# An attention and feed-forward kernel: the stack copies on two queues, the reading of folded maxima held until the division ahead is done, tensor steps taken first in a turn, and the first projections in another order

## The chip, the cores and the metric

The kernel runs on one core of one Trainium2 chip. The metric is device time in microseconds (us) of one execution, of which the median over several runs is taken. The engines are named as in the profile: PE (matrix multiply; PEld is its weight load), DVE (VectorE), ACT (ScalarE), POOL (GpSimd) and SP (SyncE, which here only issues DMAs). A trailing q, as in SPq, marks an engine's own instruction queue.

## The reference

The block is a normalised attention and a normalised gated feed-forward, each added to its input. B is 4, S is 1024, D is 256, 16 heads of 16, hidden width 1024; all in float32. The feed-forward weights hold only -1, 0 and 1, with a scale for each output row.

```python
def attn(x, Wqkv, Wout):                      # x: (4, 1024, 256)
    q, k, v = split_heads(x @ Wqkv.T)         # 16 heads of 16
    scores = einsum('bhqd,bhkd->bhqk', q, k) / sqrt(16)
    p = exp(clip(scores - max(scores), -50, 50))
    out = einsum('bhqk,bhkd->bhqd', p / (sum(p) + 1e-6), v)
    return merge_heads(out) @ Wout.T

def ffn(x):
    h = silu(x @ w1.T * s1) * (x @ w2.T * s2)
    h = gelu(h @ h1.T * t1)
    h = gelu(h @ h2.T * t2)
    return h @ w3.T * s3

x = x + layernorm(attn(layernorm(x), Wqkv, Wout))
x = x + layernorm(ffn(layernorm(x)))
```

## The kernel before

**Attention.** It fills roughly the first half of the span. Work goes by batch `b`, group `g` of four heads, and half `h` of 512 queries; such a triple is a *unit*, and there are 32. A unit has 16 tiles: eight chunks `c` of 128 keys, twice two heads. For one tile PE makes the scores of two heads in PSUM (`s`, L534), and ACT takes the exponential of 128x1024 values (`e`, L535) into a ring of eight. PE then weighs the values (`acc`, L542) with `vaug`, which holds the group's values with a column of ones, so that the sum of the exponentials comes out beside the output.

**Stacks.** Queries and keys are kept as a high and a low part (`cq`, with the low part made by DVE in L394), so that one matmul of 64 rows makes the four products of parts. For that the parts of a group's heads must lie below one another in the tiles `sq` and `sk` (`stacks`). They get there by DMA: `copies` gives 16 copies for the keys and 16 for the queries of a group (L482), 64 KB each; `stack(b, g)` turns these 32 into steps. There are two sets of stacks, used by turns (`g % 2`), so the copies of a group start when the group two before it is done (`unit_end`). For `g` of 2 or 3, the first copy has to follow the projection of the second half of the channels (`later["qk1"]`).

**Maxima and division.** The reference adds 1e-6 to the sum of exp(score - max), while the kernel's exponentials are taken without the maximum, so the small term has to be scaled by the largest exponential. DVE keeps a running maximum over the first 128 queries of each half (`top`, L554). `divide` then writes `top` to DRAM by SP (L572), reads it back turned into `folded` (step `back`, L575), folds it on DVE (L579, L580) and divides (step `run`: `em` in L584, `den`, then `on` in L565). `folded` has one buffer; `o` and `top` have two.

**Order of the work.** Instructions stand in each engine's queue in the order in which the program emits them. A loop emits in *turns*: in each, the scores and exponentials of three tiles, some of the weighing, and then `side.take`, which fits in side work: the next batch's layer norm, transposes (`pt`), projections (`p`, `pv`), flags (`pn`), the output projection (`py`), the divisions, the stack copies, and the rounding of the feed-forward weights on POOL. Side work stands in chains of `Step`s. A step has a gap in turns to the one before, may be a tensor step (at most one of these a turn, all through one PSUM bank, `misc`), may have an amount of DVE work that counts against the turn's room, and may have a condition `ready`. `take` goes through the chains in order, divisions first (`self.first`), and runs what is due.

**Queues.** SP issues the stack copies, the loads of `x` and of the output weights `wo` (L222), and both DMAs of a division. POOL computes `rstd` of each layer norm (L107), copies values to `vaug` (`slots`, L512), and loads, rounds and stores the feed-forward weights (`round_weights`, L270 to L275, and `round_corners`, L291 to L312).

**The head.** Before the loop, the first batch's layer norm, transposes and the projections of the first group are written out by hand. `queues` there deals the copies to ACT, POOL and SP: of each eight, one, four and three. The Q part of the weights is packed by `compact(0)` on ACT, emitted ahead of the first Q projection. The first `v[0]` is emitted before the loop; `v[1]` and the first `slots` are side work.

The feed-forward part, from some 590 us on, runs from a list of its own and is not touched.

Of the kernel before, what the change touches and what calls it, by code (L numbers as in the profile page):

```python
# [21 lines left out]
DH = 16  # L22
# [15 lines left out]
NQ = 512  # L38
# [91 lines left out]
def tile_fast(ctx: ExitStack, tc: tile.TileContext, x, wqk, wv, wo, w1, w1s, w2, w2s, h1, h1s, h2, h2s, w3, w3s, out, bad):  # L130
# [65 lines left out]
    with ExitStack() as actx, ExitStack() as rctx:  # L196
# [11 lines left out]
        def compact(w):  # L208
            nc.scalar.copy(wqk_sb[:, :, w], padded[:, :, w, :, 0:DH])  # L209
# [8 lines left out]
        def load_rest():  # L218


            def load(out, in_):
                return lambda: nc.sync.dma_start(out=out, in_=in_)  # L222

            def load_half(b, h):
                return lambda: load_x(b, [h])

            rest = [load_half(2, h) for h in range(NH)]
            for c in range(DC):
                for h in range(HPT):
                    r = SLOT * (HPT * c + HPG * (h % GPT) + h // GPT)  # L230
                    rest.append(load(wo_sb[DH * h : DH * (h + 1), c, :], wo[r : r + DH, :]))
            rest += [load_half(b, h) for b in range(3, B) for h in range(NH)]
            rest += [load(scales[name], w) for name, w in (("w1", w1s), ("w2", w2s), ("h1", h1s), ("h2", h2s))]
            return rest + [load(w3s_sb, w3s.partition_broadcast(P))]
# [253 lines left out]
        def few(run_all, n):  # L488


            def some(part):
                return lambda: [run() for run in part]

            return [Step(some(run_all[i : i + n]), 1, False) for i in range(0, len(run_all), n)]

        def stack(b, g):

            outstanding.append((b, g))

            def done():  # L500
                stacked[g % 2] = b, g
                outstanding.remove((b, g))

            steps = few([lambda copy=copy: copy(nc.sync) for w in (1, 0) for copy in copies(g, w)], 4 if g < GPT or later["qk1"] == b else 6)
            steps[0].ready = lambda: g < GPT or later["qk1"] == b
            return steps + [Step(done, 0, False)]

        def slots(b, g, t0=0, t1=NT):


            def run():
                nc.gpsimd.tensor_copy(  # L512
                    vaug[g % 2][:, t0:t1, :, 0:DH], cv[:, t0:t1, HPG * DH * g : HPG * DH * (g + 1)].rearrange("p t (h e) -> p t h e", e=DH)
                )
                slotted[g % 2] = b, g, t1

            return run
# [38 lines left out]
        def quotients(g, h, em, o):  # L556

            o = o.rearrange("p (j s) -> p j s", s=SLOT)
            den = small.tile([P, NQ // SLOT], F32, tag="den", name="den")
            n = P // SLOT  # L560
            nc.vector.scalar_tensor_tensor(den[:, 0:n], em, SM_EPS, o[:, 0:n, DH], ALU.mult, ALU.add)
            nc.vector.tensor_copy(den[:, n:], o[:, n:, DH])
            nc.vector.reciprocal(den, den)
            e = DH * (g % GPT)
            nc.vector.tensor_mul(on[h][:, g // GPT, :, e : e + DH], o[:, :, 0:DH], den.unsqueeze(2).to_broadcast([P, NQ // SLOT, DH]))  # L565

        def divide(g, h, o, top):


            there = shuffle.tile([HPG, P, P], F32, tag="top", name="top_d")  # L570
            folded = work.tile([P, P // SLOT, P], F32, tag="folded", name="folded", bufs=1)
            nc.sync.dma_start(out=there.rearrange("i k q -> k i q"), in_=top.rearrange("p u n q -> p (u n) q"))  # L572

            def back():
                nc.sync.dma_start(out=folded, in_=there.rearrange("i (k s) q -> (i k) s q", s=P // SLOT))  # L575

            def fold():
                for n in (2, 1):
                    nc.vector.tensor_max(folded[:, 0:n], folded[:, 0:n], folded[:, n : 2 * n])  # L579
                nc.vector.transpose(folded[:, 1], folded[:, 0])  # L580

            def run():
                em = small.tile([P, P // SLOT], F32, tag="em", name="em")
                nc.vector.tensor_reduce(em, folded[:, 1].rearrange("p (j k) -> p j k", k=SLOT), AX.X, ALU.max)  # L584
                quotients(g, h, em, o)

            return [Step(back, 2, False), Step(fold, 2, False, work=1.2), Step(run, 1, False, work=1.4)]

        def divide_last(g, h, o, top):

# [88 lines left out]
        class Side:  # L679
# [34 lines left out]
            def take(self, room=math.inf, spare=0.0):  # L714

                self.slot += 1
                free, heavy = True, False
                step = self.next_tensor(self.slot)

                self.room = min(self.room, 0.5) + room - (step.work if step and not step.heavy else 0)  # L720
                for chain in self.first + self.rest:
                    while (step := self.due(chain, self.slot, free)) and (step.tensor or not step.work or self.room > spare):
                        chain[0].pop(0)
                        chain[1] = self.slot
                        if step.split:
# [600 lines left out]
        normalise = [steps[: TPQ // 2] for steps in xt]  # L1326
        for step in norm[0] + normalise[0] + norm[1]:
            step.run()
        for h in range(NH):
            for step in xt[h][TPQ // 2 :]:  # L1330
                step.run()
            for w, step in zip((1, 0), qk[0][h]):
                if (h, w) == (0, 0):
                    compact(0)
                step.run(0, 1)
                for i, copy in enumerate(copies(0, w, h * NQ, (h + 1) * NQ)):
                    copy(queues[i % len(queues)])
                if w and h + 1 < NH:
                    for step in normalise[h + 1]:
                        step.run()  # L1340
        stacked[0] = 0, 0
        v[0].run()
        alone = False
        load_x(1)
        early = [v[1], Step(slots(0, 0, 0, NT // 2), 0, False)]
        side.add(early + v[2:] + [Step(slots(0, 0), 0, False), Step(slots(0, 1), 0, False)] + sum(qk[1], []) + [Step(lambda: later.update(qk1=0, v=0), 0, False), Step(lambda: add_flags(flags[0] + flags[1]), 0, False)])
# [293 lines left out]
```

## Time and profile before

| what | us |
|---|---|
| median of 3 runs | 1218.02 |
| the runs | 1216.05 to 1218.22 |
| the profiled execution | 1217.59 |
| its span, first to last instruction | 1215.7 |
| PE, ACT, DVE, POOL busy | 1162.8, 885.8, 841.0, 207.8 |
| first exponential starts | 27.35 |

The busy times tell how much of the span an engine has work; a busy PE is also one whose matmuls run slowly. In an answer on waits, each line gives the waiting engine and line, what it waited for, and us in total, how often, and the longest. In a timeline a line gives start and duration in us, engine, line, instruction, what it writes and reads, its shapes and count, and in brackets the idle time of the engine before it and what ended it. A line of a table by stretches gives the busy time of each engine with the number of its instructions, then the granted clock of PE as a share of full speed, the DMA engines' busy share and GB/s.

### The profile page before, as it was taken

To read this page: it belongs to the slowest core of one execution; us is meant where nothing else is said; L and a number is where in the kernel's file an instruction comes from. 1 tells how busy PE (TensorE), PEld (TensorE's weight loads), DVE (VectorE), ACT (ScalarE), POOL (GpSimd) and SP (SyncE) were. 2 spreads that over 40 slices of the span, in tenths; PEclk is the share of its full clock that TensorE was granted. 3 is DMA by queue.
4 is the path that set the end of the run, shared out by engine and by line. 5 is a ranking of instruction groups with operands and counts; after the bars stand their busy time and mean duration, and the time that the engine had idled before them with its cause. 6 is when DMAs were issued, how large, how long until landed. Compare 5 with 4: busy or idle time off the path is not lost.

```text
span 1215.7 us, 21265 instructions
## 1 busy us (share of the span) xinstructions
PE 1162.8 (96%) x7994; PEld 708.4 (58%) x7994; DVE 841.0 (69%) x1500; ACT 885.8 (73%) x1049; POOL 207.8 (17%) x279
## 2 busy tenths in 40 slices
PE   7899999999999999999999999999999999999995
PEld 2333333333333333333478889888898887988885
DVE  3485668777687756867775757767669576695756
ACT  3798899878989989999456565675756757556661
POOL 6221135435354432100010000000000000000000
PEclk9999999999999999999999999999999999999998
DMA  4776755756666765454304442254523536135411
GB/s 136 179 184 159 166 149 133 189 133 171 158 152 165 187 170 141 92 138 148 105 1 140 138 139 77 97 169 144 188 72 99 176 124 201 60 104 173 142 50 38
DMA packets 78672, 163.66 MB, mean 135 GB/s; under 512 B 14688, under 2 KB 40928, under 8 KB 78560
## 3 DMA queue, kind: packets, MB, share of 16 engines
q1 hardware_dynamic: 68624, 131.27, 39.3%
q0 software_dynamic: 9408, 30.42, 7.9%
q8 instruction: 65, 1.06, 0.4%
q10 hardware_dynamic: 528, 0.52, 0.2%
q14 instruction: 47, 0.39, 0.1%
HBM read 98.71 MB, written 29.88 MB: 106 GB/s over the span
## 4 chain that ended last, share of the span: by engine, by line
PE 69%; ACT 10%; DVE 9%; DMA 4%; SPq 3%; issue 3%; ACTq 0%; POOL 0%; POOLq 0%; DVEq 0%
PE ph L1034 34%; PE acc L542 10%; PE pg L955 8%; ACT e L535 8%; PE s L534 6%; PE pz L1142 4%; PE p L321 3%; SPq L482 2%; DVE top L554 2%; PE py L321 2%; DMA x<-in_x_dram 1%; PE pv L321 1%; DMA sq<-cq1lo 1%; DVE st L97 1%; PE fpt L898 1%
## 5 line engine op out<-in xcount | busy, mean ns | idle before, releaser
L535 ACT ACTIVATE e<-s 128x1024 f32<-128x1024 f32 x512 | 483.0, 1044 | 52.5 <-PE s L534 42.8
L542 PE MATMUL acc<-e,vaug 128*32 128x512 f32 (+1 forms) x2424 | 259.0, 540 | 3.2 <-POOL vaug L512 3.2
L534 PE MATMUL s<-sq,sk 64*128 64x512 f32 x1024 | 189.2, 446 | 24.0 <-ACT e L535 17.8
L534 PEld LDWEIGHTS s<-sq,sk 64*128 64x128 f32 x1024 | 87.4, 185 | 170.7 <-ACT e L535 141.8
L1034 PE MATMUL ph<-hi,sq 128*128 128x512 f32 x448 | 177.7, 397 | 0.0
L1034 PE MATMUL ph<-lo,sq 128*128 128x512 f32 x448 | 176.7, 394 | 0.0
L1034 PE MATMUL ph<-hi,sk 128*128 128x512 f32 x448 | 176.6, 394 | 0.0
L1034 PE MATMUL ph<-lo,sk 128*128 128x512 f32 x448 | 176.4, 394 | 0.0
L107 POOL TENSOR_TENSOR rstd<-ve,minus_half 128x4 f32<-128x4 f32 (+1 forms) x34 | 38.2, 1123 | 729.8 <-DVE ve L105 625.4
L554 DVE TENSOR_TENSOR top<-top,e 128x512 f32<-128x512 f32 x192 | 138.9, 723 | 24.5 <-ACT e L535 18.7
L542 PEld LDWEIGHTS acc<-e,vaug 128*32 128x32 f32 x2424 | 62.0, 110 | 121.0 <-issue 108.2
L929 DVE TENSOR_TENSOR lo<-g,hi 128x1024 fp32r<-128x1024 f32 x48 | 58.8, 1225 | 58.1 <-ACT hi L925 58.0
L1034 PEld LDWEIGHTS ph<-lo,sk 128*128 128x128 f32 x448 | 84.1, 188 | 20.0
L1034 PEld LDWEIGHTS ph<-hi,sk 128*128 128x128 f32 x448 | 84.1, 188 | 20.0
L1034 PEld LDWEIGHTS ph<-hi,sq 128*128 128x128 f32 x448 | 84.1, 188 | 19.5
L1034 PEld LDWEIGHTS ph<-lo,sq 128*128 128x128 f32 x448 | 84.2, 188 | 19.3
L1022 ACT ACTIVATE c<-ph,h_scale 128x512 f32<-128x512 f32 x64 | 40.6, 685 | 55.7 <-PE ph L1034 55.7
L929 DVE TENSOR_TENSOR lo<-c,hi 128x1024 fp32r<-128x1024 f32 x48 | 58.2, 1219 | 25.8 <-ACT hi L925 25.8
L957 ACT ACTIVATE sg<-pg,w_scale 128x512 f32<-128x512 f32 x64 | 43.9, 688 | 42.0 <-PE pg L955 38.4
L321 PE MATMUL p<-xT,wqk_sb 128*32 128x512 f32 x512 | 67.4, 606 | 4.5 <-ACT wqk_sb L209 2.6
L958 DVE SCALAR_TENSOR_TENSOR g<-pg,w_scale,sg 128x512 f32<-128x512 f32 x64 | 47.7, 747 | 22.1 <-ACT sg L957 22.1
L1142 PE MATMUL pz<-w_sb,hi 128*128 128x256 f32 x256 | 60.0, 279 | 0.0
(183 smaller groups left out, 1729.0 us busy)
## 6 DMA issues: line engine op xcount, KB each, us to landing
sq<-h_f SPq DMA_DIRECT2D x56, 512.0 KB, 3.7
sk<-h_f SPq DMA_DIRECT2D x56, 512.0 KB, 4.4
w<-in_h_dram POOLq DMA_DIRECT2D x32, 256.0 KB, 5.2
h_f<-wr POOLq DMA_DIRECT2D x16, 512.0 KB, 4.3
x<-in_h_dram SPq DMA_DIRECT2D x16, 512.0 KB, 3.5
top_d<-top SPq DMA_DIRECT2D x30, 256.0 KB, 2.4
folded<-top_d SPq DMA_DIRECT2D x30, 256.0 KB, 3.2
h_f<-wr POOLq DMA_DIRECT2D x16, 384.0 KB, 3.8
```

The lines of the kernel that those rows point to most:

```text
L321: nc.tensor.matmul(o[j : j + SLOT, :], w[:, j : j + SLOT], i, **flags)
L534: nc.tensor.matmul(s[:, a, :], stacks[1, g % 2, u][r, c * P : (c + 1) * P], stacks[0, g % 2, u][r, h * NQ : (h + 1) * NQ], start=True, sto ...
L535: nc.scalar.activation(pair(k)[:, u], s, AF.Exp)
L542: nc.tensor.matmul(acc[SLOT * i : SLOT * (i + 1), q0:q1], vaug[g % 2][:, c, i, :], pair(k)[:, i // 2, i % 2, q0:q1], start=c == 0 and q0 = ...
L554: nc.vector.tensor_max(top, top if c > 1 else pair(k - 2)[:, :, :, 0:P], pair(k)[:, :, :, 0:P])
L929: nc.vector.tensor_sub(self.lo[i].t, self.raw[i].t, self.hi[i].t.bitcast(F32))
L955: nc.tensor.matmul(p[:, k, :], homes[n][d][:, m * P : (m + 1) * P], half[:, d, :], start=d == j == 0, stop=d == DC - 1 and j == 1)
L957: nc.scalar.activation(sg, p[:, 0, :], AF.Silu, scale=scales["w1"][:, m : m + 1])
L958: nc.vector.scalar_tensor_tensor(x[i, h][c // 2].t[:, c % 2, :], p[:, 1, :], scales["w2"][:, m : m + 1], sg, ALU.mult, ALU.mult)
L1022: nc.scalar.activation(o.t[:, j, :], (o.t if src is None else src)[:, j, :], AF.Gelu, scale=scale[:, m : m + 1])
L1034: nc.tensor.matmul(p[:, j, :], w, half, start=start and c == n == 0, stop=c == HC // 2 - 1 and n == 1, skip_group_check=True,)
L1142: nc.tensor.matmul(p[:, j, :D], half[:, (t0 + j) * P : (t0 + j + 1) * P], homes["w3"][c], start=c == order[0] and n == 0, stop=c == order[ ...
```

## The change

- `stack`: the 32 copies go to SP, POOL, SP and so on by turns, six in a step; before, all went to SP, and a step had four or six.
- `load_rest`: the 16 loads of `wo` are issued by POOL, not SP.
- `divide`: the step that reads the maxima back waits, by a condition, until the division of the unit ahead has been emitted.
- `take`: chains whose next step is a tensor step are gone through first, then all chains as before.
- The head: `compact(0)` is emitted before the first K projection, the normalisation of the second half is split around that projection, ACT's copies of the first Q are emitted after the second half's transposes, `v[1]` is emitted before the loop, and the first group's `slots` run on DVE in two halves (the copy for the second group stays on POOL).

```diff
-            def load(out, in_):
-                return lambda: nc.sync.dma_start(out=out, in_=in_)
+            def load(out, in_, queue=nc.sync):
+                return lambda: queue.dma_start(out=out, in_=in_)
...
-                    rest.append(load(wo_sb[DH * h : DH * (h + 1), c, :], wo[r : r + DH, :]))
+                    rest.append(load(wo_sb[DH * h : DH * (h + 1), c, :], wo[r : r + DH, :], nc.gpsimd))
...
-            steps = few([lambda copy=copy: copy(nc.sync) for w in (1, 0) for copy in copies(g, w)], 4 if g < GPT or later["qk1"] == b else 6)
+            turns = (nc.sync, nc.gpsimd, nc.sync)
+            runs = [copy for w in (1, 0) for copy in copies(g, w)]
+            steps = few([lambda copy=copy, queue=turns[i % len(turns)]: copy(queue) for i, copy in enumerate(runs)], 2 * len(turns))
...
-        def slots(b, g, t0=0, t1=NT):
+        def slots(b, g, t0=0, t1=NT, engine=nc.gpsimd):
...
-                nc.gpsimd.tensor_copy(
+                engine.tensor_copy(
...
+        divided = {"made": 0, "done": 0}
+
         def divide(g, h, o, top):
...
+            mine = divided["made"]
+            divided["made"] += 1
...
                 quotients(g, h, em, o)
-
-            return [Step(back, 2, False), Step(fold, 2, False, work=1.2), Step(run, 1, False, work=1.4)]
+                divided["done"] += 1
+
+            begun = Step(back, 2, False)
+            begun.ready = lambda: divided["done"] == mine
+            return [begun, Step(fold, 2, False, work=1.2), Step(run, 1, False, work=1.4)]
...
-                for chain in self.first + self.rest:
+                chains = self.first + self.rest
+                for chain in [c for c in chains if c[0] and c[0][0].tensor] + chains:
...
-        for h in range(NH):
+
+        def project_first(h, w):
+
+            qk[0][h][1 - w].run(0, 1)
+            runs = [(queues[i % len(queues)], copy) for i, copy in enumerate(copies(0, w, h * NQ, (h + 1) * NQ))]
+            for queue, copy in runs:
+                if queue is not nc.scalar:
+                    copy(queue)
+            return [copy for queue, copy in runs if queue is nc.scalar]
+
+        def turn_first(h):
+
             for step in xt[h][TPQ // 2 :]:
                 step.run()
-            for w, step in zip((1, 0), qk[0][h]):
-                if (h, w) == (0, 0):
-                    compact(0)
-                step.run(0, 1)
-                for i, copy in enumerate(copies(0, w, h * NQ, (h + 1) * NQ)):
-                    copy(queues[i % len(queues)])
-                if w and h + 1 < NH:
-                    for step in normalise[h + 1]:
-                        step.run()
+
+        turn_first(0)
+        compact(0)
+        normalise[1][0].run()
+        for copy in project_first(0, 1):
+            copy(nc.scalar)
+        normalise[1][1].run()
+        held = project_first(0, 0)
+        turn_first(1)
+        for copy in held:
+            copy(nc.scalar)
+        for w in (1, 0):
+            for copy in project_first(1, w):
+                copy(nc.scalar)
         stacked[0] = 0, 0
-        v[0].run()
+        for step in v[0:2]:
+            step.run()
+        slots(0, 0, 0, NT // 2, nc.vector)()
         alone = False
         load_x(1)
-        early = [v[1], Step(slots(0, 0, 0, NT // 2), 0, False)]
-        side.add(early + v[2:] + [Step(slots(0, 0), 0, False), Step(slots(0, 1), 0, False)] + sum(qk[1], []) + ...
+        side.add(v[2:] + [Step(slots(0, 0, NT // 2, NT, nc.vector), 0, False), Step(slots(0, 1), 0, False)] + sum(qk[1], []) + ...
```

More of the change, by code (lines that the diff above doesn't have):

```diff
@@ L1328, in tile_fast @@
             step.run()
-        for h in range(NH):
+        def project_first(h, w):
[6 more added lines that the diff above has]
+        def turn_first(h):
             for step in xt[h][TPQ // 2 :]:
                 step.run()
-            for w, step in zip((1, 0), qk[0][h]):
-                if (h, w) == (0, 0):
-                    compact(0)
-                step.run(0, 1)
-                for i, copy in enumerate(copies(0, w, h * NQ, (h + 1) * NQ)):
-                    copy(queues[i % len(queues)])
-                if w and h + 1 < NH:
-                    for step in normalise[h + 1]:
-                        step.run()
+        turn_first(0)
[11 more added lines that the diff above has]
+                copy(nc.scalar)
         stacked[0] = 0, 0
-        v[0].run()
+        for step in v[0:2]:
+            step.run()
+        slots(0, 0, 0, NT // 2, nc.vector)()
         alone = False
         load_x(1)
-        early = [v[1], Step(slots(0, 0, 0, NT // 2), 0, False)]
-        side.add(early + v[2:] + [Step(slots(0, 0), 0, False), Step(slots(0, 1), 0, False)] + sum(qk[1], []) + [Step(lambda: later.update(qk1=0, v=0), 0, False), Step(lambda: add_flags(flags[0] + flags[1]), 0, False)])
+        side.add(v[2:] + [Step(slots(0, 0, NT // 2, NT, nc.vector), 0, False), Step(slots(0, 1), 0, False)] + sum(qk[1], []) + [Step(lambda: later.update(qk1=0, v=0), 0, False), Step(lambda: add_flags(flags[0] + flags[1]), 0, False)])
         begin(0)
```

## The prediction

> **What bounds the kernel now.** I read the page's busy times first, then the waits of TensorE, then the timeline at each long wait.
>
> ```profile
> PE 1162.8 (96%) x7994; PEld 708.4 (58%) x7994; DVE 841.0 (69%) x1500; ACT 885.8 (73%) x1049; POOL 207.8 (17%) x279
> ...
> L535 ACT ACTIVATE e<-s 128x1024 f32<-128x1024 f32 x512 | 483.0, 1044 | 52.5 <-PE s L534 42.8
> ```
>
> PE is busy 96% of the span. The attention stage runs from the first exponential at 27.35 us to the last, which ends near 591 us; after it, the windows show PE busy at 50.00 of 50 us almost throughout, so the feed-forward stage cannot give or take much. In attention, 512 exponentials have 483 us of ACT; ACT waits for PE more than for anything else. PE runs one program in a fixed order, so **the stage is the sum of PE's work and PE's idle time**. What the change can win is idle PE time, and matmuls that ran at a lower clock. The waits of PE name it:
>
> ```profile
> PE s L534 <- DMA sq<-cq1lo: 5.3, 3, 2.8
> PE acc L542 <- POOL vaug L512: 3.2, 2, 1.6
> PE p L321 <- ACT wqk_sb L209: 2.6, 1, 2.6
> PE py L321 <- DVE norm L426: 2.1, 2, 1.8
> ```
>
> Columns: total us, times, longest. (The larger PE wait, 17.8 us in 52 pieces of some 0.4 us for ACT's exponentials, is the normal hand-over and stays.) The timeline puts the four in place. The head, with the idle time before each in brackets:
>
> ```profile
> 14.94 3.43 PE L321 MATMUL p<-xT,wqk_sb 128*32 128x512 f32 x16 [2.63 <-ACT wqk_sb L209]
> 18.30 1.23 PE L363 MATMUL pt<-ident,xn 128*128 128x128 f32 x8
> ...
> 32.38 1.06 PE L542 MATMUL acc<-e,vaug 128*32 128x512 f32 x8 [1.61 <-POOL vaug L512]
> ```
>
> The first Q projection waits for `compact(0)`, which sits on ACT behind two DMA issues, and takes 3.43 us; the K projection before it, of the same 16 matmuls, took 1.92. Then two late stacks:
>
> ```profile
> 83.95 3.14 SPq L482 DMA_DIRECT2D sq<-cq1hi  x4
> 87.14 0.57 SPq L222 DMA_DIRECT2D wo_sb<-in_wo_dram  x1
> ...
> 99.87 1.07 PE L534 MATMUL s<-sq,sk 64*128 64x512 f32 x2 [1.88 <-DMA sq<-cq1lo]
> ...
> 229.19 3.39 SPq L482 DMA_DIRECT2D sq<-cq1lo  x4
> 240.04 0.33 SPq L575 DMA_DIRECT2D folded<-top_d  x1
> 240.42 2.41 SPq L482 DMA_DIRECT2D sq<-cq1hi  x4
> 242.88 2.50 SPq L482 DMA_DIRECT2D sq<-cq1lo  x4
> ...
> 246.70 0.47 PE L534 MATMUL s<-sq,sk 64*128 64x512 f32 x1 [2.77 <-DMA sq<-cq1lo]
> ```
>
> These are two causes. From 69.69 to 98.56 SP issues without a pause (32 stack copies, seven loads of `wo`, three DMAs of divisions): SP itself is full. From 232.6 to 240.04 SP stands still in front of L575, which overwrites `folded` while the unit before has not read it (L584 ran at 239.74); eight copies wait behind it. Both times the clock drops:
>
> ```profile
> 98.00:104.00 6.00, 4.12 (x20) 1.36 (x22) 4.57 (x14) 3.05 (x4) 0.00 (x0) 0.72 0.27 55
> 244.00:251.00 7.00, 4.13 (x21) 1.30 (x21) 3.68 (x10) 2.96 (x3) 0.00 (x0) 0.76 0.53 100
> ```
>
> The column after POOL is the granted clock: 0.28 x 6 and 0.24 x 7 us are 1.7 us lost each, on top of the idle time.
>
> **What the Trainium skill says.** "TensorE: Matmul & The Clock Gate", What's actually happening: a lightly used window of 3.4 us lets the clock fall to half. The trace agrees: three falls in the stretch up to 251 us, each next to a PE wait of 1.88 to 2.77 us, each worth 1.7 us. "DMA: Bandwidth & Descriptors", SWDGE vs HWDGE vs iDMA: a DMA on POOL has its descriptors written by the GpSimd cores. "SBUF — State Buffer", Who interferes with whom: POOL is shut out while certain VectorE operations run. The trace of before shows only mildly longer POOL issues: 0.487 us for the head's copies, 0.54 to 0.81 for the weight DMAs later.
>
> **The change, part by part.**
>
> *Head.* `compact(0)` moves ahead of the first K projection's copies: ACT ends the second `xT` at 10.82, compacts by 11.5, so Q's matmuls follow K's at 12.3 and, with PE busy, at full clock: done by 14.3. The second half's `xn` is split around the K residual: its `rstd` is there at 12.74, then half of 1.42 us, L394's 0.69, the other half: 14.9. So the transposes start at 14.9, not 18.30: **3.4 us**. From there the old distances hold, since the held ACT issues (1.2 us) now follow `xT`. The Q copies must be there when PE, after v[0] and v[1], reaches the scores near 25 us: POOL has 8 + 8 copies of 0.49 us from 13.3, so 21.1, plus 2.2 to land, 23.3; SP's 6 + 6 of 0.6 land near 23.7. Just in time. v[1] is only moved. The values go to `vaug` on DVE, idle there, not on POOL behind 16 copies: the 1.61 us vanish, and about 0.8 of the later 1.56 us (POOL began 0.13 us after `cv`, copied twice for 1.95). With 0.3 for a wait on `cv`: head **6.1 us**.
>
> *Stack copies.* 15 stacks of 32 copies. Before: 4 a turn in 8 turns, all on SP at 0.59 to 0.69 us. After: 21 on SP, 11 on POOL, 6 turns. SP's share per turn stays at 4, but ends two turns (some 6.5 us) earlier; 16 `wo` loads leave it too. The stall at 98 (1.88 + 1.7) and one of 0.62 at 136.7 go: **4.2 us**. POOL takes 165 copies and 16 loads: 181 x 0.49 to 0.81 = 89 to 147 us, on an engine with under 12 of each 20 us busy: hidden, if its order allows (rivals).
>
> *`begun.ready`.* L575 is not issued before the other division was; SP no longer stands in front of it and nothing is added to SP. The late stack at 244: 2.77 + 1.7 = **4.5 us** (the earlier copies would cover part of this too; I count it once). The wait it adds is in the order of emission: the unit's division comes later, and with it `o` and `top`, both with two buffers; 0, while a unit is about 17 us and one division 5 turns.
>
> *Tensor steps first.* PE gets the same number of steps; what alters is DVE's order in a turn: PSUM is emptied ahead of the division and statistics.
>
> ```profile
> 343.75 1.93 PE L321 MATMUL py<-wo_sb,oT 128*32 128x256 f32 x32 [1.84 <-DVE norm L426]
> ```
>
> Here L426 waited behind em, den, `on` and two statistics (340.43 to 343.0) with the one misc bank held: **1.8 us** gone. The order was not seen elsewhere; bound it by -2 to +4 us (another such stall with its clock).
>
> Sum: 6.1 + 4.2 + 4.5 + 1.8 = 16.6 us. A new order of 500 turns makes some new wait: I charge one of the kind at 98, 3.6 us. Net **13 us**. The profiled execution took 1217.59 us (span 1215.7), 0.4 below the median 1218.02. 1217.6 - 13 = **1204.6**.
>
> **Rivals.**
>
> *POOL delivers late (slower).* POOL runs in order, and waits:
>
> ```profile
> 169.36 0.72 POOL L309 TENSOR_TENSOR wr<-w 128x256 fp32r<-128x256 f32 x1 [3.79 <-DMA h_f<-wr]
> ...
> 253.20 0.61 POOL L512 COPY vaug<-cv 128x512 f32<-128x512 f32 x1 [14.23 <-PE acc L542]
> ```
>
> At 253.20 POOL is 5 us behind SP's first copy (248.42), then has 4.7 us of `sums`. A stack's last POOL copy comes 5 + 6 turns of 3.3 + about 4 to land: 29 us of the 35 from SP's first copy to the group's first exponential (283.35). Slack 6 us: against it speaks that; for it, that 3.79 us waits come once per corner of h1 and h2. If POOL is more than 6 us later still, a group pays about 2.8 + 1.7. That decides the sign when more than 16.6/4.5, four, of the 15 groups do; at five or six, 1220 to 1225. `rstd` behind the copies (2 a turn, 1 to 1.6 us) would join it.
>
> *Only the head and half of the stalls.* Idle PE is pushed to where ACT is short: it is busy for 19.27 of the 20 us from 60 and 18.85 of those from 80. Against it speaks that it has 15.60 and 14.12 in the 20 us slices of the two stalls. Then 6.1 plus 2 to 4: 1208 to 1212.
>
> *It does not do what it says.* The readiness test binds only where a division is late (one wait of 7.7 us in L575), and the tensor order may pick the same steps; with a head whose scores wait for the Q copies, 2 us or less are left: 1216.
>
> **How the numbers follow.** The forecast (at most one or two new stalls, 1198 to 1208) has 0.63; half of it 0.20; no effect 0.06; POOL late 0.11. Low end: the whole 16.6, and 2 more from the tensor order with up to 2 in the head: 1197. High end: into the second case's worse side, 1213. About 0.2%, 2.4 us, is what a measurement can tell here. Faster by more: 0.84; within: 0.05; slower: 0.11.
>
> **What would show it.** First exponential near 25.5 us, Q's 16 matmuls in 1.9 us, no PE wait for `vaug`; no long PE wait on a stack; the last copy of a stack 10 us before its group; no SP gap in front of L575; the clock at 1.00 between 20 and 580 us. A PE wait for a copy that POOL issued, or VectorE waiting for `rstd` beyond 1.2 us, would prove the forecast wrong.

## The result, and the profile after

| what | before | after |
|---|---|---|
| median of the runs taken together | 1218.12 (4 runs, 1216.05 to 1218.39) | 1207.53 (4 runs, 1206.14 to 1208.69) |
| the profiled execution | 1217.59 | 1206.14 |
| its span | 1215.7 | 1204.4 |
| first exponential starts | 27.35 | 24.17 |
| last exponential ends | 590.70 | 576.67 |
| last `z` ends (end of the computed output) | 1210.09 | 1196.19 |

The change makes the kernel faster: ratio 0.991, 95% interval 0.9889 to 0.9931, or 10.6 us by the medians. The forecast was 1204.6 us, range 1197 to 1213. The forecast's time is 2.9 us too low, and the sum behind it holds errors, shown below, that cancel in part. The profiled execution after is the fastest of its four, so what the two traces show side by side comes out a little larger than the difference of the medians.

The page's busy times, as before: engine, us, share of the span, number of instructions; and the row of the exponentials.

```profile
PE 1160.6 (96%) x7994; PEld 709.1 (59%) x7994; DVE 845.9 (70%) x1501; ACT 886.2 (74%) x1050; POOL 298.7 (25%) x458
...
L537 ACT ACTIVATE e<-s 128x1024 f32<-128x1024 f32 x512 | 483.0, 1046 | 43.8 <-PE s L536 34.1
```

The number of matmuls is the same and PE is busy 2.2 us less, while ACT waits for PE's scores 8.7 us less (42.8 to 34.1). POOL has 90.9 us more work, at the low end of the 89 to 147 us that the prediction gave to its 181 DMAs. The waits of PE, shown as before (total us, times, longest):

```profile
PE s L536 <- ACT e L537: 19.5, 50, 2.9
...
PE acc L544 <- DVE o L798: 1.4, 3, 1.0
PE pn L424 <- DVE cv L327: 0.8, 1, 0.8
...
PE s L536 <- DMA sq<-cq0hi: 0.4, 1, 0.4
```

All four lines that carried the prediction are gone: no wait of 5.3 us on a stack, none for `vaug`, `wqk_sb` or `norm`. What is left on a stack is 0.4 us in the head. The first line grew by 1.7 us, and its longest piece from 1.8 to 2.9 us; both stand at the same place, in the last unit of attention (a_split below). The head in PE's timeline (start, duration, and the idle time before in brackets):

```profile
10.45 3.64 PE L321 MATMUL p<-xT,wqk_sb 128*32 128x512 f32 x32 [0.25 <-ACT xT L324]
14.02 1.62 PE L363 MATMUL pt<-ident,xn 128*128 128x128 f32 x8
...
23.43 0.70 PE L536 MATMUL s<-sq,sk 64*128 64x512 f32 x2 [0.44 <-DMA sq<-cq0hi]
...
29.04 1.07 PE L544 MATMUL acc<-e,vaug 128*32 128x512 f32 x8
```

K and Q are one block of 32 matmuls in 3.64 us, 16 in 1.82; before, Q alone took 3.43 after an idle 2.63. The second half's transposes start at 14.02, not 18.30, and weighing starts without a wait for `vaug`. Windows (start:end, length, busy us of PE, PEld, DVE, ACT and POOL, then the clock, DMA share, GB/s) around the places of the three late waits of before:

```profile
92.00:98.00 6.00, 5.86 (x44) 2.45 (x44) 5.82 (x16) 6.00 (x7) 0.81 (x2) 1.00 0.00 0
232.00:240.00 8.00, 8.00 (x72) 3.20 (x70) 5.12 (x12) 7.47 (x9) 1.13 (x3) 1.00 0.43 122
325.00:331.00 6.00, 6.00 (x70) 2.49 (x66) 5.66 (x15) 5.48 (x7) 5.70 (x9) 1.00 0.60 155
```

PE has no hole and the clock is at 1.00 in all three. Before, the clock fell at 15.2, 100.5, 247.3 and 585.2 us; after, only at 570.9. Each fall lasted 3.41 us at half the clock, so it cost at most 1.7 us, and three fewer are at most 5.1 us of the gain.

**Where the time went.** I took the start of each unit, the first exponential of its sixteen, in both traces; the lead is the difference. Units are written b,g,h. Later I call this table the ledger.

| place | before | after | lead | step of the prediction |
|---|---|---|---|---|
| first exponential | 27.35 | 24.17 | 3.2 | head |
| end of the first unit | 48.67 | 43.12 | 5.55 | head, `vaug` |
| start of 0,2,1 | 118.91 | 110.06 | 8.85 | stall at 98 |
| start of 1,1,1 | 224.59 | 216.15 | 8.44 | 1.25 more won by 0,3,1, then 1.6 given back |
| start of 1,2,1 | 266.19 | 252.11 | 14.08 | stall at 244 |
| start of 2,1,0 | 354.56 | 338.82 | 15.74 | stall at 342 (unit 2,0,1: 19.33 to 17.33) |
| end of the last exponential | 590.70 | 576.67 | 14.03 | given back, 1.2 in the last unit |
| end of the last `z` | 1210.09 | 1196.19 | 13.9 | |
| end of the program | 1215.73 | 1204.35 | 11.4 | nothing in the prediction |

The first lines flatter the head. In this execution of before PE waits 1.46 us at 8.4 for the first `xn`, in this one of after 0.2. Over all kept traces the first unit ends at 46.41 to 48.67 with the old head (five traces) and at 41.98 to 44.92 with the new (nine), 4.5 us apart on average.

The last line is the surprise. 2.5 us of the lead are lost after the output has been computed, where the change edits nothing. One answer for the closing line of each kernel, in which the engines drain (shortest/median/longest in ns, first and last start):

```profile
L1636 POOLq DRAIN  x3: 50/98/3172, 1211.0 to 1215.5; - x3
```

```profile
L1664 POOLq DRAIN  x3: 50/107/6516, 1197.0 to 1204.1; - x3
```

The first is before, the second after. POOL's closing DRAIN grew from 3.17 to 6.52 us. Before, it ended at 1214.2, ahead of SP's own closing DRAIN at 1214.9; after, it ends at 1203.5, 2.7 us behind SP's at 1200.8, and is what the program ends on. From the end of the last `z` to the end of the program are 5.65 and 8.16 us.

### The profile page after: what moved, and what is told of

Its sections match the earlier page's. It is cut to its first block, busy times and chain, and to the rows that moved or that the text cites. A ratio compares the mean times of both kernels' runs of the same rounds, so it can differ in the third digit from the quotient of the medians.

```text
span 1204.4 us, 21320 instructions
## 1 busy us (share of the span) xinstructions
PE 1160.6 (96%) x7994; PEld 709.1 (59%) x7994; DVE 845.9 (70%) x1501; ACT 886.2 (74%) x1050; POOL 298.7 (25%) x458
## 3 DMA queue, kind: packets, MB, share of 16 engines
q0 software_dynamic: 15200, 41.50, 12.6%
## 4 chain that ended last, share of the span: by engine, by line
PE 71%; DVE 10%; ACT 9%; issue 4%; DMA 3%; SPq 2%; POOL 1%; ACTq 0%; POOLq 0%; DVEq 0%
PE ph L1045 35%; PE acc L544 10%; PE pg L966 9%; ACT e L537 8%; PE s L536 7%; PE pz L1153 4%; PE p L321 2%; DVE top L556 2%; PE py L321 2%; SPq L482 1%; PE pv L321 1%; DVE st L97 1%; DMA x<-in_x_dram 1%; DMA sq<-cq0hi 1%; PE fpt L909 1%
## 5 line engine op out<-in xcount | busy, mean ns | idle before, releaser
L537 ACT ACTIVATE e<-s 128x1024 f32<-128x1024 f32 x512 | 483.0, 1046 | 43.8 <-PE s L536 34.1
L556 DVE TENSOR_TENSOR top<-top,e 128x512 f32<-128x512 f32 x192 | 140.1, 730 | 21.1 <-ACT e L537 15.4
```

Of the source, the lines that this page charges most:

```text
L537: nc.scalar.activation(pair(k)[:, u], s, AF.Exp)
L556: nc.vector.tensor_max(top, top if c > 1 else pair(k - 2)[:, :, :, 0:P], pair(k)[:, :, :, 0:P])
```

## The experiments

Twelve more kernels were timed, in three sets; each set has its own times of the kernel before (medians 1219.39, 1219.73, 1219.13). All ratios are to these; the change stands at 0.991. A difference between two ratios is uncertain by about 0.003, 3.6 us, since each interval reaches about 0.002 to either side. I give differences in us as the difference of ratios times 1219.

### One part undone at a time

**a_sp**: all copies of a stack on SP, still six to a turn; `wo` stays on POOL.

```diff
-            turns = (nc.sync, nc.gpsimd, nc.sync)
+            turns = (nc.sync, nc.sync, nc.sync)
```

> After, with all stack copies on SP, still six to a turn; the wo loads stay on POOL. Theory (a full SP queue made the late stacks near 98 and 137 us, and POOL's many DMAs lengthen its closing DRAIN): the scores of the third group wait again, 1.9 us and 1.7 us of clock, and a little at the fourth, so the attention stage is 3.5 to 5 us longer than after, while POOL's closing DRAIN falls from 6.5 us back to about 3.2 us, so the end comes only 1 to 2.5 us later than after. Rival (six to a turn and the wo loads' move were what mattered, the second queue not): no wait on a stack comes back, and the kernel is 2 to 3 us faster than after by the shorter DRAIN. A third view, that the DRAIN has nothing to do with POOL's DMAs: DRAIN stays at 6.5 us.

Measured: 1.0091 [1.0063, 1.012], 1228.05 us: **slower than before**, and 22 us slower than the change. Six copies of 0.6 us are 3.6 us of SP in a turn of some 3.3, so SP falls behind the program. SP's own queue, then DVE's timeline, then the longest waits of DVE:

```profile
410.96 2.48 SPq L482 DMA_DIRECT2D sq<-cq1lo  x4
413.54 1.45 SPq L576 DMA_DIRECT2D top_d<-top  x1
420.22 0.33 SPq L582 DMA_DIRECT2D folded<-top_d  x1
```

```profile
422.94 0.75 DVE L586 TENSOR_TENSOR folded<-folded 128x256 f32<-128x256 f32 x2 [4.55 <-DMA folded<-top_d]
...
424.53 0.67 DVE L426 TENSOR_REDUCE norm<-pn 64x4 f32<-64x512 f32 x1
```

```profile
DVE folded L586 <- DMA folded<-top_d: 24.3, 10, 6.4
```

The write of the maxima, L576, comes directly behind 18 copies issued without a pause (from 401.69). Here it also lands slowly, 6.7 us after its issue, where the page of after has a median of 2.5 (before has one such, 7.4 us at 120.78). The read, L582, waits 5.1 us for it. DVE, in order, stands 4.55 us in front of L586, and `norm` (L426) runs late behind it, for which PE then waits 2.67 us at 425.26. In the longest of DVE's waits, 6.42 us at 137.15, the maximum is ready at 128.53, and SP gets to its write only at 131.93. DVE's wait for `folded` is 24.3 us in ten pieces, where it was 3.7 in three before and 1.6 in one after. So six to a turn is affordable only with the second queue (a_sp4 below undoes the step size as well). Neither theory had the size: both thought of late copies, of which there is one (2.41 us of PE's time at 133.15), and neither of the division that stands behind copies. The closing DRAIN is 3335 ns here, with 16 POOL DMAs more than before, as the theory said.

**a_noready**: the condition on `back` left out.

```diff
-            begun.ready = lambda: divided["done"] == mine
```

> After, without the condition on the step that reads the maxima back. Theory (SP standing in front of that DMA made the late stack at 244 us): the gap on SP in front of it comes back, near 220 to 235 us, but two turns' earlier copies cover a part, so the scores of that group wait 0 to 2.8 us; 0 to 4.5 us slower than after. Rival (the earlier copies alone cure it): SP's gap comes back and no PE wait follows; within 1 us of after. If the condition carries the whole of the 5.2 us by which the unit at 244 became shorter, 5 us slower.

Measured: 0.9915 [0.9897, 0.9934], 1208.85: 0.6 us above the change, not to be told from nothing. SP's queue:

```profile
221.92 0.55 SPq L482 DMA_DIRECT2D sq<-cq1lo  x1
232.86 0.33 SPq L582 DMA_DIRECT2D folded<-top_d  x1
```

SP does stand still before L582 for 10.4 us, as it did in before, but the copy ahead of the gap is the stack's last. PE waits for no stack. With the condition the gap is there too, 221.70 to 231.00, and does no harm either. The earlier copies had already cured the stall at 244: unit 1,2,0 takes 17.65 us here, 17.02 in after and 22.19 in before.

**a_notensor**: the chains in the old order.

```diff
-                for chain in [c for c in chains if c[0] and c[0][0].tensor] + chains:
+                for chain in chains:
```

> After, with the chains gone through in the old order. Theory (the order of DVE's work in a turn kept the one misc bank held at 342 us): the PE wait of about 1.8 us for norm comes back near 328 us, and the kernel is about 2 us slower than after. Rival (the order makes as many waits as it removes): within 1 us, with the PE waits of 0.8 to 1.0 us that after has at 133 and 204 us gone.

Measured: 0.9921 [0.9903, 0.9939], 1209.05 (1207.2 to 1214.52): 1.3 us, within the uncertainty. The waits of PE show what the order is for:

```profile
PE py L321 <- DVE norm L426: 2.4, 2, 1.6
PE acc L544 <- DVE o L798: 2.2, 1, 2.2
PE pn L424 <- DVE cv L327: 1.6, 1, 1.6
```

The wait for `norm` is back, 1.64 us at 334.8, beside a wait of 2.2 for `o`; after has 1.4 for `o` in three pieces. The third wait, for `cv`, is 0.8 in after. b_stack, the other kernel with two queues and the old order, has this one of 1.6 too; with a fall of the clock beside it, both take 21.8 us for unit 0,3,0, where the six kernels with two queues there and the new order take 18.1 to 18.9. The profiled execution was the slowest of its six, so I use its waits and single units and not its span.

The lengths of some units go with the order alone, whatever else differs between the kernels (us, from the first exponential of the unit to that of the next):

| unit | old order: before, a_notensor, the four b kernels | tensor steps first: after, the seven other a kernels |
|---|---|---|
| 2,0,1 | 19.11 to 20.95 | 17.27 to 17.86 |
| 1,0,0 | 17.11 to 17.39 | 17.92 to 18.41 |
| 1,1,0 | 16.71 to 17.16 | 17.17 to 18.03, a_noready 19.73 |
| 3,3,1 | 18.95 to 19.69 | 20.25 to 20.92, without a_split and a_few_split |

So the order wins some 1.8 us in 2,0,1, and loses about 0.6, 0.7 and 1.2 us in the other three (after against a_notensor). These losses are most of what the ledger lists as given back.

**a_oldhead**: the head as in before, all else as after.

```diff
-        turn_first(0)
-        compact(0)
-        normalise[1][0].run()
...
-        slots(0, 0, 0, NT // 2, nc.vector)()
+        for h in range(NH):
...
+            for w, step in zip((1, 0), qk[0][h]):
+                if (h, w) == (0, 0):
+                    compact(0)
+                step.run(0, 1)
```

> After, with the old head. Theory (the head saves PE's idle time before the first exponentials and for vaug, and PE stays the bound until the end): the first exponential near 27.4 us, the first unit 2 us longer, and the kernel 5 to 6 us slower than after. Rival (what the head saves is lost again in later units where ACT is short): the first exponential 3.2 us later, the end less than 3 us later.

Measured: 0.9952 [0.9935, 0.9969], 1212.25: 5.1 us slower than the change. PE's waits in the head are those of before:

```profile
PE acc L544 <- POOL vaug L514: 3.2, 2, 1.7
PE p L321 <- ACT wqk_sb L209: 2.6, 1, 2.6
```

The head is worth 5 us in the company of the other parts, close to the lead of 5.55 at the end of the first unit.

### One part done at a time

**a_sp4**: the copies on SP alone, and in steps of four, as before.

```diff
-            turns = (nc.sync, nc.gpsimd, nc.sync)
+            turns = (nc.sync, nc.sync, nc.sync)
...
-... enumerate(runs)], 2 * len(turns))
+... enumerate(runs)], 4 if g < GPT or later["qk1"] == b else 6)
```

> After, with all stack copies on SP and the old step size of four. Theory (with six copies a turn on one queue SP needs 3.6 us of a 3.3 us turn, falls behind, and the reading of the maxima lands late, so that VectorE waits for it; with four, 2.4 us, SP keeps up): VectorE waits for folded 2 to 6 us in total, not 24; the late stack near 98 us may come back; 1212 to 1217 us, between after and before. Rival (it is the number of copies that SP must issue, not how many a turn): as slow as with six, 1225 us or more.

Measured: 0.9964 [0.9947, 0.998], 1216.06: 6.6 us slower than the change. The waits on stacks are larger than they were in before:

```profile
PE s L536 <- DMA sq<-cq1lo: 4.9, 4, 2.3
PE s L536 <- DMA sq<-cq0lo: 3.4, 2, 2.4
```

They stand at 60.56 (2.42), 131.46 (2.32) and 279.69 (1.66), not at 98. What the head saves is lost where the faster PE meets the next stack earlier than SP can deliver it. With four to a turn DVE hardly waits for the division any more, which confirms the cause found in a_sp:

```profile
DVE folded L586 <- DMA folded<-top_d: 2.6, 3, 2.0
```

And unit 1,2,0 takes 17.02 us here with SP alone: the condition is enough for the stall at 244, as the second queue is.

**b_stack** (before, plus the two queues with six to a turn, and `wo` on POOL), **b_ready** (before, plus the condition) and **b_head** (before, plus the head).

```diff
+            turns = (nc.sync, nc.gpsimd, nc.sync)
...
+... enumerate(runs)], 2 * len(turns))
```

> Before, with the stack copies dealt to SP and POOL, six to a turn, and the loads of wo on POOL; nothing else changed. Theory (the second queue is the part that carries the stacks, both the late one at 98 and the one at 244 us): both PE waits on stacks gone, minus 8 us in attention, plus 2.5 us by POOL's longer closing DRAIN: 5 to 6 us faster than before. Rival (the gain near 244 us needs the condition as well): only the wait at 98 us gone, 1 to 2 us faster than before.

Measured: 0.9955 [0.9938, 0.9972], 1213.61, a gain of 5.5 us. PE has no wait on a stack in the whole trace, so this part **cures the stalls at 98 and at 244 both**. The waits for `wqk_sb`, `vaug` and `norm` stay, a wait of 1.6 us for `cv` comes in unit 0,3,0 (21.76 us, 19.29 in before), and the closing DRAIN is 6.52 us. The 5.5 us are what is left after these losses.

```diff
+            begun = Step(back, 2, False)
+            begun.ready = lambda: divided["done"] == mine
```

> Before, with the condition on the step that reads the maxima back; nothing else changed. Theory of the prediction (SP no longer stands in front of that DMA): the PE wait at 246.7 us and its clock fall gone, 4.5 us faster than before. Rival (SP alone cannot deliver that stack in time even without standing still, because it is full): the wait shrinks by less than half, within 2 us of before.

Measured: 0.9959 [0.9944, 0.9974], 1213.91, a gain of 5.0 us. SP's queue:

```profile
231.20 3.79 SPq L482 DMA_DIRECT2D sq<-cq1hi  x4
235.03 2.49 SPq L482 DMA_DIRECT2D sq<-cq1lo  x4
239.68 0.33 SPq L580 DMA_DIRECT2D folded<-top_d  x1
```

The eight copies that came at 240.42 in before now run at 231.20 to 237.5, ahead of the read. The wait at 244 is gone; those at 95.7 (3.15 us) and 136 (0.83) stay:

```profile
PE s L534 <- DMA sq<-cq1lo: 4.4, 3, 3.1
```

Alone, the condition is worth what the prediction said, 4.5; beside the second queue it is worth 0.6, not to be told from nothing, because both cure the same stall.

```diff
+        turn_first(0)
+        compact(0)
+        normalise[1][0].run()
...
+        slots(0, 0, 0, NT // 2, nc.vector)()
```

> Before, with the new head alone (its slots on DVE included). Theory (PE stays the bound, so what the head saves stays saved): first exponential near 24 us, 5 to 6 us faster than before. Rival (the first group's stacks of the next unit were timed to the old head, so SP, whose work is not shortened, is later against PE): the head's 5 us are met by longer PE waits on stacks at 60 and 95 us, and 2 us or less are left.

Measured: 0.9991 [0.9977, 1.0005], 1216.87: about 1 us, not to be told from nothing, although the first exponential starts at 23.55, 3.8 us earlier. PE's waits:

```profile
PE s L534 <- DMA sq<-cq1lo: 6.8, 3, 3.1
PE p L321 <- DVE xT L327: 2.6, 1, 2.6
```

Waits on stacks grow from 5.3 to 6.8 us (3.10 at 96.09, 2.64 at 244.29), and a new wait of 2.6 stands at 76: DVE makes that `xT` behind L579, which stands 2.74 us for a read of the maxima that SP issued at 69.31 and that took 6.8 us to land. By the starts of the units the lead over before is 5.7 us at 0,1,0, 1.9 at 0,1,1 and 0.3 at 0,2,1; so more of it goes at 76 than at the stack at 98. Both hang on DMAs that SP issues, and an earlier head does not bring these forward as far: the read lands at 76.12, in before at 76.79. The single gains are 1.1 + 5.5 + 5.0, 11.6 us without the tensor order, and look additive to the 10.6 of the whole; but the parts are not independent. The head keeps its lead only with the second queue (a_sp4, b_head), and the queue and the condition share one stall.

### The end of the program

**b_drain**: before, with 144 POOL DMAs of 64 KB added in the feed-forward stage, where POOL has time. They copy rows of `h1` to a scratch tensor that nothing reads.

```diff
+            scratch = dram.tile([16 * 48 * 3, HID], F32, name="scratch")
...
+                if b:
+                    for g in range(NH * HC):
+                        for i in range(3):
+                            steps[g].append(lambda r=..., k=...: nc.gpsimd.dma_start(out=scratch[r : r + 16, :], in_=h1[k : k + 16, :]))
```

> Before, with 144 DMAs of 64 KB more, issued by POOL in the feed-forward stage from DRAM to a scratch tensor that nobody reads. Theory (POOL's closing DRAIN grows with the DMAs that POOL has issued): DRAIN 6 to 6.6 us instead of 3.17, and the end 2 to 3 us later after the last output is computed. Rival (the longer DRAIN of after comes from something else, such as the copies' SBUF side or the place of the code): DRAIN stays near 3.2 us.

Measured: 1.003 [1.0017, 1.0043], 1222.84: 3.7 us slower. The closing line:

```profile
L1641 POOLq DRAIN  x3: 46/98/6847, 1214.6 to 1222.0; - x3
```

From the end of the last `z` to the end are 8.63 us, 3.0 more than before. The attention stage is emitted as in before and still the DRAIN has doubled: it comes with the DMAs that POOL issued, and it shows at the end.

**a_few**: the second queue only where SP is full: batch 0, and the last group of batch 1. The other stacks are on SP, four to a turn. The expectation counts 40 POOL copies; the kernel has 44.

```diff
+            mixed = b == 0 or (b, g) == (1, NG - 1)
+            turns = (nc.sync, nc.gpsimd, nc.sync) if mixed else (nc.sync,)
...
+... enumerate(runs)], 6 if mixed else 4)
```

> After, with copies on POOL only for the four stacks at which SP alone was late in the runs so far (groups 1 to 3 of the first batch, group 3 of the second); the others go to SP, four to a turn. POOL issues 40 stack copies, not 150. Theory: POOL's closing DRAIN 4.0 to 4.4 us, so the end 2.2 us closer to the last output, no new wait on a stack: 1.5 to 2.5 us faster than after. Rival (the other stacks come late on one queue with this order of the work): one or two PE waits on stacks come back, and it is not faster than after.

Measured: 0.9906 [0.9885, 0.9928], 1207.29, the change's ratio within 0.0004. The closing line and the waits of PE on stacks:

```profile
L1665 POOLq DRAIN  x3: 50/98/3907, 1197.6 to 1202.1; - x3
```

```profile
PE s L537 <- DMA sq<-cq1lo: 1.2, 2, 0.7
PE s L537 <- DMA sq<-cq0lo: 1.1, 1, 1.1
```

The DRAIN is back to 3.91 us, and from the last `z` to the end are 5.54, 2.6 us less than after. But waits on stacks are there again, 1.1 us at 337.4 and 0.73 at 406.8. In the times no gain can be told from the change; the rival was right.

**a_split**: the piece of 2.9 us in PE's wait for the exponentials. For the last unit but one, 3,3,0, `divide_last` does the whole division on DVE in one step. DVE's, ACT's and PE's timeline of after:

```profile
562.98 0.70 DVE L605 STREAM_TRANSPOSE turned<-top 128x512 f32<-128x512 f32 x1
...
566.73 0.42 DVE L567 TENSOR_TENSOR on<-o,den 128x256 f32<-128x256 f32 x1
567.08 0.68 DVE L556 TENSOR_TENSOR top<-e,e 128x512 f32<-128x512 f32 x1
...
567.85 2.85 ACT L537 ACTIVATE e<-s 128x1024 f32<-128x1024 f32 x3 [3.92 <-DVE top L556]
...
568.93 0.50 PE L536 MATMUL s<-sq,sk 64*128 64x512 f32 x2 [2.85 <-ACT e L537]
```

DVE runs the division from 562.98 to 567.08 without a break; the new maximum (L556) frees the ring of exponentials only after it, ACT stands for 3.92 us, PE for 2.85. The window from 566 to 575 has a clock of 0.81, 1.7 us more. Before had the same in a smaller size: ACT stood 2.69 us and PE 1.78, with a fall at 585.2. All six kernels of the old order have 1.78 or 1.79 for PE here, and all six of the new order with this division in one step have 2.85 to 2.87, so the difference comes from the tensor order. DVE shows why: in after, `em` to `on` of the division ahead (559.23 to 560.54) stand behind a step that waits 2.80 us for PE; in before they ran ahead of it (570.27 to 571.57), and it waited 1.57. The experiment cuts the step in three and changes nothing else.

```diff
-            return [Step(run, 1, False)]
+            if h == NH - 1:
+                return [Step(lambda: (turn(), gather(), run()), 1, False)]
+            return [Step(turn, 1, False), Step(gather, 1, False), Step(run, 1, False)]
```

> After, with the last group's division (first half of the queries) emitted in three steps in as many turns, not in one. Theory (in after, ACT waits 3.9 us at 567 us because the running maximum stands behind 4 us of that division on DVE, and PE then 2.85 us with a fall of the clock): the PE wait near 566 us falls under 1 us, 3 to 4.5 us faster than after. Rival (the stage's end is set by ACT and the weighing anyway): the wait moves to the next turns, within 1 us of after.

Measured: 0.9875 [0.9853, 0.9898], 1204.29: 4.3 us better than the change by the ratios, 3.2 by the medians. The same place:

```profile
565.45 0.69 DVE L608 TENSOR_REDUCE top<-turned 128x16 f32<-128x512 f32 x1
566.06 0.68 DVE L556 TENSOR_TENSOR top<-e,e 128x512 f32<-128x512 f32 x1
...
566.83 5.61 ACT L537 ACTIVATE e<-s 128x1024 f32<-128x1024 f32 x6 [1.16 <-DVE top L556]
```

The maximum slips in behind the first third; ACT waits 1.16 us, PE has no wait over 0.41 us from 560 to 572, and the clock from 564 to 573 is 1.00. The last unit takes 16.47 us instead of 20.60, 4.1 us less, about what the medians and ratios show.

**a_few_split**: both edits.

```diff
+            mixed = b == 0 or (b, g) == (1, NG - 1)
...
+            return [Step(turn, 1, False), Step(gather, 1, False), Step(run, 1, False)]
```

> After, with both: copies on POOL for four stacks only, and the last division in three steps. If both theories hold, the gains add up, since one is at the end of the program and the other at the end of attention: 5 to 6.5 us faster than after, near 1201 us. If one of them fails, only the other's share.

Measured: 0.9874 [0.9852, 0.9897], 1203.71, with a DRAIN of 3.91 us. It is the lowest median of all, but not to be told from a_split. By the ratios it is 4.4 us better than the change, short of the 5 to 6.5 expected: the part with the DRAIN adds nothing that can be told. Both beat before and, by the ratios just outside their uncertainty, the change.

## Why the prediction was right, and where its sum was wrong

**The bound.** "The stage is the sum of PE's work and PE's idle time" held: PE executes the same 7994 matmuls, and each of the four PE waits named as removable is gone in after.

**Head, 6.1 us.** Measured 5.55 in the ledger, 4.5 as the mean of all traces, 5.1 with the part undone. The steps stand: transposes at 14.02 (the prediction worked out 14.9), no `vaug` wait, first exponential at 24.17 (it said 25.5). What the step left out is its condition: alone, the head gives 1 us (b_head), since the DMAs that SP issues for the next units come too late for it. The prediction priced it "from there the old distances hold"; they hold only with the second queue.

**Stack copies, 4.2 us.** The two stalls went as said; the ledger has 3.5 at 98 and 1.25 up to 0,3,1. But b_stack shows that this part also removes the wait at 244, which the prediction booked under the next item. Its sentence "SP's share per turn stays at 4" names the quantity that decides: a_sp, with six on SP, is 22 us slower, and 15.5 of these go with the step size (a_sp4).

**`begun.ready`, 4.5 us.** The size is right for the stall (5.2 in unit 1,2,0 of the ledger, 5.0 alone in b_ready), the **attribution is wrong**: in the change's company the condition is worth 0.6, within the uncertainty (a_noready). The prediction saw the overlap, "the earlier copies would cover part of this too; I count it once". Counting it once kept the sum right. That the copies cover all of it could have been worked out: six to a turn on two queues end two turns earlier, and before the gap at 232.6 to 240.04 that is enough.

**Tensor steps first, 1.8 us.** The ledger has 2.0 in unit 2,0,1, and the table by order has 1.8 or so in every kernel, so the stall and its size are shown. "The order was not seen elsewhere" is where the step was short: the order also spares the two-queue kernels the wait for `cv` in 0,3,0, and costs 0.6 to 1.2 us in three other units. What it is worth in all, 1.3 us by the ratios, is less than the uncertainty. On before alone it was not tried.

**The sum.** 16.6 forecast, against a largest lead of 15.75. The 3.6 charged for one new wait stood for 1.6 given back in batch 1 and 1.7 after the start of 2,1,0, of which 1.2 in the last unit. That the amount fits is luck: the charge named no place, and what came was several small losses, most of them made by the tensor order. In the last unit it is 1.1 us on top of a wait that before had too (PE 1.78, now 2.85), each with its clock fall (585.2 and 570.9), and not a whole new wait "of the kind at 98". So up to the last `z` the lead is 13.9, where the forecast had 13.

**The step that failed** is "181 x 0.49 to 0.81 = 89 to 147 us, on an engine with under 12 of each 20 us busy: hidden". The duration was right (POOL +90.9 us) and the issues were hidden. The cost of POOL's DMAs at the end of the program was not: 2.5 us of the closing DRAIN (6.52 us in all six kernels with the 181 DMAs, 3.17 in the three without any of them; b_drain 6.85 with no other change). 13.9 less 2.5 is the 11.4 us of the profiled spans; by the medians it is 10.6.

**The rivals.** *POOL delivers late* did not happen: no PE wait on a copy that POOL issued. The last copy of a stack lands 2.8 to 10.3 us ahead of its group's first exponential (83.93 to 93.56 for group 2 of batch 0, 227.03 to 235.09 for group 2 of batch 1; the shortest is POOL's, 336.06 to 338.82 for group 1 of batch 2), where in before three landed behind it. So the slack of 6 us that the rival had was mostly there, and once it was half of that. Its sum is off: five or six late groups, 4.5 us each, less the 16.6 come to 1223.5 to 1228 and not 1220 to 1225. Its side remark on `rstd` came true once; DVE in after:

```profile
DVE y L126 <- POOL rstd L107: 4.3, 3, 3.1
```

The 3.1 us end at 385.28, where POOL stands 2.48 us in front of the store of a rounded weight (L294) and `rstd` comes behind it; in before this gap is 0.30. PE does not wait for it. *Only the head and half of the stalls* and *it does not do what it says* are refuted by the ledger; what a lone head does (b_head) is the second rival's picture.

**The signs.** Seen: Q's matmuls, no `vaug` wait, no long wait on a stack. In part: the last copy 10 us ahead of its group holds for seven of 15 stacks by the end of its issue, for one by its landing. A sign against the forecast was seen too, VectorE's wait of 3.1 us for `rstd` ("beyond 1.2 us"); it cost PE nothing, so it was badly chosen. Not seen: "no SP gap in front of L575" (now L582): the gap is there, 9.3 us at 231.00, but with nothing behind it, so this sign was badly chosen as well. "The clock at 1.00 between 20 and 580" holds but for the fall at 570.9. What the Trainium skill says in "TensorE: Matmul & The Clock Gate", What's actually happening, which the prediction cites for the falls, agrees with a_split: where the long wait near 566 is taken out, the fall goes with it. But the length of one wait does not decide alone: before has no fall beside 1.84 us at 343.75, and a_split has one at 25.87 beside 1.38 us, where after has none beside 1.27.

## What to carry to other kernels

When two parts of a change cure the same stall, price them alone and together: the sum may be right and each price wrong, and a part that finishes sooner (here the head) is worth little until the queue that feeds what follows keeps pace. A new order of emission can win in one unit and lose in others: compare the lengths of the same unit over all kernels with and without it. A queue's budget is issues per turn times its issue time against the turn, and what overruns first may be another client of that queue, here the division's DMAs. Work moved to an idle engine can be hidden all along and still be paid for at the end of the program: follow both traces to the last instruction, not only to the last output.

## What the hardware showed that I had not expected

- POOL's closing DRAIN grows with DMAs that it issued long before: 3.17 us in before, 3.34 with 16 more (a_sp), 3.91 with 60 more (a_few: 44 copies, 16 `wo`), 6.52 with 181 more (after, b_stack), 6.85 with 144 more between two DRAM tensors (b_drain). It follows neither the number of POOL's DMAs alone nor their packets (14016 in b_drain, 15200 in after). b_drain's last POOL DMA is issued at 1084 us, that of the others by 529; whether that matters was not settled.
- With two queues at work each copy lands later: SP's 64 KB copies had medians of 2.4 to 2.9 us from issue to landing before, and 3.5 to 4.3 after; those on POOL took 3.7 to 5.1. Six to a turn on SP alone (a_sp) gave 2.5 to 3.1, so it is the second queue and not the larger step. The Trainium skill, "DMA: Bandwidth & Descriptors", SWDGE vs HWDGE vs iDMA, has the GpSimd cores write the descriptors of POOL's DMAs; the issue on POOL is nevertheless short here, 0.484 to 0.670 us, against a median of some 0.59 on SP.
- The Trainium skill, "SBUF — State Buffer", Who interferes with whom, has POOL shut out during some operations of VectorE. With DVE busy 70% of the span, no issue of a stack copy on POOL took longer than 0.670 us, so it did not bear on them.
